# Self-attention on one core: key blocks met in a ring instead of a triangle, accumulation rounds dealt out beforehand, context products two steps late

## The chip, the cores and the metric

The kernel runs on one core of one Trainium2 chip. The metric is the device time of one execution in microseconds. The engines are PE (TensorE, matrix products; PEld is its weight load), DVE (VectorE), ACT (ScalarE), POOL (GpSimd) and SP (SyncE, which here issues every transfer between DRAM and SBUF). Each engine works through its own instructions in order and waits on semaphores of the others.

## The reference

The model takes four images of 128 channels and 64 x 64 positions through a mixer with convolutions and a state space scan, a convolution, then (on 4096 tokens of 128 channels per image) an attention with a small feed-forward part, an expert layer, a linear attention and a second expert layer. The change touches the first attention alone. Cut to what matters, it is, for x of shape (4, 4096, 128) with H = 16 heads of D = 8:

```python
qkv = _qz_ring(heads + rx_theta)            # running products of cosines, 8 numbers per token and head
q = jnp.transpose(qkv, (0, 2, 1, 3))        # (B, H, S, D)
scores = jnp.einsum('bhsd,bhtd->bhst', q, q) / np.sqrt(D)
attn = jax.nn.softmax(scores, axis=-1)
ctx = jnp.einsum('bhst,bhtd->bhsd', attn, q)
attn_out = ctx @ w_comb.T + b_comb
x1 = _ln(x + attn_out, g1, beta1)
zf = jnp.cos(x1[..., :NQ_FFN]) * jnp.cos(ry_theta)
h = jax.nn.relu(zf @ w1.T + b1)
ffn_out = h @ w2.T + b2
return _ln(x1 + ffn_out, g2, beta2)
```

Queries, keys and values are the same numbers, so the matrix of scores is symmetric: exp(score) of a block of queries against a block of keys, transposed, is that of the second block's queries against the first block's keys.

## The kernel before, in words

`layer2_attention` runs over the four images. For each one `prepare` computes q for all heads and stores it to DRAM (`head_d` for queries and keys, `value_d` for the values of the transposed half), while `feed_forward` finishes the image before. Then `attention` works alone. After the last image `feed_forward` runs by itself. What follows is `attention`.

The 4096 tokens make NJ = 4 blocks of 1024. In block j of head h, the queries of block j meet keys in steps: a step (h, j, m) takes the m-th pair of 128-key tiles, so m runs from 0 to 15 and m // 4 is the block of the keys. A step is *own* if m // 4 = j. If it lies in another block, it is called *met* here (`behind` in the code), and its exponentials are used twice. Block j meets all later blocks: block 0 has 12 met steps and 4 own ones, block 1 has 8 and 4, block 2 has 4 and 4, block 3 has only 4 own ones. `pairs` mixes them: in block 0 three met steps and an own one in turn, in block 1 two and one, in block 2 one and one. `blocks` puts block 3 of the head before between blocks 0 and 1. A head has 40 steps, 24 of them met.

One step does this, in the program's order:

- PE: four `score` products into two PSUM half-tiles (`sps`, L90 through the helper `mm`; the pool `pssc` has three half-tiles).
- PE: `turns(...)`, some *rounds* of products for the transposed half (`acc_ps`). A *group* is the four met steps of one (h, j, i), i being the block of the keys; its transposed exponentials fill a tile `turned` (two buffers), and eight rounds of four products each weigh them with the values of block j. `turns` computes at every step how many rounds are due (at least 1, at most 3) and stops if the group's last step is not two steps old. In the trace one product of these is two instructions, so a round is 8 instructions of `acc_ps`, and a step's context product 8 of `ctx_ps`.
- DVE: the second transpose of the met step before (L1197).
- PE: `weigh`, the context product of the step before: exp (`ex`) against the values `qt` into `ctx_ps`. At a block's end, for j > 0, it adds the transposed sums of earlier blocks by eight products with `place`; DVE copies ctx_ps (L1140), and SP stores it in eight transfers to `num_d` and `den_d`.
- DVE: sums of folded exponentials that are ready (L1204).
- ACT: two exps (L1211), each 128 x 1024. In a met step the row sums are needed too: either ACT writes them (`accum_out`, an extra read of its accumulator), or the step is put *aside*: POOL folds the exps twice (L1158, L1159) and DVE sums the rest. `folded` puts 11 of the 24 met steps aside.
- DVE: the first transpose of a met step (L1217).

The exps of a step lie in one of four buffers `ex`. A finished group's PSUM half is copied or added by DVE into `accs[h]` (L1089, L1091). When the last group of a block is done, the values of the block after next are loaded (`load_values`, four loads of L1022, tile `v`); three steps later POOL spreads them (`spread_values`, L1030, `turned_v`). The keys and queries of the next head come by 32 loads (L903) from block 1's first step on, and POOL rounds them (L912) 11 and 15 steps later.

PE, DVE and POOL keep the program's order in `attention`. The order of SP and ACT, and which of the four `ex` buffers a step gets, is decided by the framework's scheduler.

Of the kernel before, what the change touches and what calls it, by code (L numbers as in the profile page):

```python
# [17 lines left out]
P = 128  # L18
# [806 lines left out]
def layer2_attention(K, xd, dpool, w):  # L825
# [6 lines left out]
    with ExitStack() as ctx:  # L832
# [47 lines left out]
        head_d = dpool.tile([2, P, L], F32, name="head_d")  # L880
        value_d = dpool.tile([NH, 32, NJ - 1, 4, BT, HD], F32, name="value_d")
        num_d = dpool.tile([2, P, L], F32, name="num_d")
        den_d = dpool.tile([2, NH, L], F32, name="den_d")
        nrm_d = [dpool.tile([P, L], F32, name=f"nrm_d{i}") for i in range(2)]

# [28 lines left out]
        def prepare(b, big, two, work, psum):  # L914
# [50 lines left out]
            def store(c):  # L965
# [3 lines left out]
                j = c // 2  # L969
                if c % 2 == 0 and j < NJ - 1:  # L970
                    laters[j] = work.tile([P, NH, BT, HD], F32, name="later", bufs=1)
                if j < NJ - 1:
                    at = laters[j][:, :, 4 * (c % 2) : 4 * (c % 2) + 4]
                    nc.gpsimd.tensor_copy(at.rearrange("p h t d -> p t h d"), cs)
                if c % 2 and j < NJ - 1:
# [30 lines left out]
        def attention(qt, first, dsum, big, two, work, pssc, psctx, psacc):  # L1006
# [6 lines left out]

            dacc = big.tile([P, NJ - 1, NH, NTT], F32, name="dacc")
            nc.gpsimd.memset(dacc, 0.0)
# [33 lines left out]
            begins, last = {}, {}  # L1049
            for n, (h, j, _) in enumerate(steps):  # L1050
                begins.setdefault((h, j), n)
                last[h, j] = n
            heads = {0: first}
            values = {(0, 0): spread_values(load_values(0, 0))}
            waiting = []
            order = [(h, j) for h in range(NH) for j in range(NJ - 1)]
# [4 lines left out]
            halves = [0]  # L1061

            def turn():

                r, h, j, i, td, _, sums = groups[0]
                if r == 0:
# [15 lines left out]
                if r < BT - 1:  # L1082
                    return False
                groups.pop(0)
                if i == 1:
                    accs[h] = work.tile([P, NJ - 1, BT, 32], F32, name="acc")
                at = accs[h][:, i - 1]
                if j == 0:
# [3 lines left out]
                if i == NJ - 1:  # L1092
                    after = order.index((h, j)) + 2
                    if after < len(order):
                        waiting.append((now[0] + 3, order[after], load_values(*order[after])))
                return True

            def turns(n, ready):


                due = left = 0
                for g in groups:
                    left += BT - g[0]
                    due = max(due, -(-left // max(1, g[5] - n + 1)))
                for _ in range(min(max(due, 1), 3)):
                    if not groups or not ready(groups[0]) or turn():
                        return

            def weigh(h, j, m, exs):

                last = m == 4 * j + 3
                first = m == (4 * j + 4 if j < NJ - 1 else 4 * j)
                for p in range(2):
                    at = (h * NTT + 2 * m + p) * (HD + 1)
                    for c in range(2):
                        mm(
                            cps[unit(p, c), :],
                            qt[:, at : at + 32],
                            exs[:, p, c, :],
                            start=first,  # L1120
                            stop=last and j == 0,
                        )
                if not last:
                    return
                if j > 0:
                    while any(g[1] == h and g[3] == j for g in groups):
                        turn()
                    for k in range(2):
                        for p in range(2):
                            for c in range(2):  # L1130
                                a = 2 * p + k
                                mm(
                                    cps[unit(p, c), :].rearrange("r (t a s) -> r t a s", a=4, s=32)[:, :, a],
                                    place[:, a, :],
                                    accs[h][:, j - 1, 4 * c : 4 * c + 4],
                                    start=False,
                                    stop=k == 1,
                                )
# [8 lines left out]

            values[order[1]] = spread_values(load_values(*order[1]))
            folds = []

            def folded(j, m):

                return ((m - 4) % 3 == 0, m % 2 == 0, m % 4 < 3)[j]

# [8 lines left out]

            starts = [n for n, (h, j, m) in enumerate(steps) if m // 4 > j and m % 4 == 0]
            ends = dict(zip(starts, [n - 1 for n in starts[2:]] + [len(steps) - 1] * 2))
            begun = {}
            turned = None
            past = None
            now = [0]
            upright = None  # L1170
            for n, (h, j, m) in enumerate(steps):
                now[0] = n
                keys, queries = heads[h]
                if j in (1, 2) and h + 1 < NH:
                    at = n - begins[h, 1]
                    if at == 0:
                        heads[h + 1] = load(h + 1, two)
                    if at in (11, 15):
                        rounded(heads[h + 1][at == 15])
                while waiting and n >= waiting[0][0]:  # L1180
                    _, at, v = waiting.pop(0)
                    values[at] = spread_values(v)
                behind = m // 4 > j
                if n in ends:
                    turned = work.tile([P, BT, 2 * CH], F32, name="turned")
                    end = min(ends[n], last[h, m // 4])
                sps = [pssc.tile([P, 2, CH], F32, name="score") for p in range(2)]
                for p in range(2):
                    for c in range(2):
# [4 lines left out]
                        )  # L1194
                turns(n, lambda g: begun[id(g[4])] < n - 1)
                if upright is not None:
                    nc.vector.transpose(*upright)  # L1197
                    upright = None
                if past is not None:
                    weigh(*past)  # L1200

# [3 lines left out]
                exs = work.tile([P, 2, 2, CH], F32, name="ex", bufs=4)  # L1205
                aside = behind and folded(j, m)
                for p in range(2):
# [3 lines left out]
                    nc.scalar.activation(  # L1211
                        ex, sps[p], AF.Exp, scale=scale, accum_out=dacc[:, j, h, t : t + 1] if summed else None
                    )
# [4 lines left out]
                if aside:  # L1218
                    fold(n, exs, dacc[:, j, h, 2 * m : 2 * m + 2])
                past = (h, j, m, exs)  # L1220
                if behind and m % 4 == 3:
                    begun[id(turned)] = n
                    groups.append([0, h, j, m // 4, turned, end, None])
            assert upright is None and not groups
            weigh(*past)
            for _, qs, at in folds:
# [3 lines left out]
        def feed_forward(b, dsum, work, psum):  # L1230

            loads, x1s, hids, sums, halves, lasts, rcs = {}, {}, {}, {}, {}, {}, {}

            def fetch(c):
# [544 lines left out]
```

## Time and profile before

| | |
|---|---|
| time, three runs | 10711.77, 10717.14, 10717.62 us; median 10717.14 |
| profiled execution, span from first to last instruction | 10707.7 us (its own time is not listed apart; the median is 9.4 above the span) |
| busy in the span | PE 8939.2, DVE 7658.7, ACT 7518.8, POOL 5247.7 us |
| mean granted TensorE clock | 0.914; 1.00 in the attention stretches |
| attention stretches, from the first score that flows on | 3328.3 to 4689.2, 4904.6 to 6264.9, 6481.5 to 7839.8, 8055.4 to 9413.6 us |
| between them (`feed_forward` and the next `prepare`) | 215.2, 216.5 and 215.5 us |

In the lines of the profile, L12 is line 12 of the kernel, and L90 is the helper through which nearly all matrix products go, so that products are told apart by the tile they write (score, acc_ps, ctx_ps). A group's line gives out<-in, shapes, how many, then busy us, mean ns of one, and the idle time of its engine just before, with what ended it. A timeline's line gives start, length, engine, line, operation, how many, and in brackets the idle time before and what released it. Work of PE, PEld and ACT overlaps at its ends, so lengths add up to more than the time that passes: distances between starts are the surer measure.

### The profile page before, as it was taken

Reading aid. Unit: us, or ns where it says so; the run is one execution under the profiler, and the core shown is the slowest. Engines: PE = TensorE matmul, PEld = TensorE weight load, DVE = VectorE, ACT = ScalarE, POOL = GpSimd, SP = SyncE. Lnnn points to the kernel's source line nnn. Section 1 sums busy time; section 2 is a strip of 40 time slices with the busy share of each in tenths; the row PEclk is TensorE's granted clock in tenths of the full one; section 3 lists DMA queues with packets and bytes.
Section 4 is the critical chain, followed back from the end, with each engine's and each line's share of the span. In section 5 each row is a group of like instructions: output and inputs, shape, how many; then the busy total and the mean of one; then the engine's idle time right before and its main releaser. Section 6 shows DMA issues by size and latency. Waiting matters only on the chain. (4 is left out here: it accounts for less than half of the span.)

```text
span 10707.7 us, 184050 instructions
## 1 busy us (share of the span) xinstructions
PE 8939.2 (83%) x71952; PEld 3434.1 (32%) x71952; DVE 7658.7 (72%) x8462; ACT 7518.8 (70%) x10323; POOL 5247.7 (49%) x3143
## 2 busy tenths in 40 slices
PE   6777777777876999988999978999978999976767
PEld 2123323322342333333333333333333333323433
DVE  2788677668856777777777777777777777754563
ACT  3565575565536999977999968999968999941431
POOL 0565555456634666545556645666646665520000
PEclk8788888878888999999999989999989999987987
DMA  3322331322212122122122222222232222123004
GB/s 82 88 72 57 86 78 48 92 70 59 62 55 57 34 34 33 33 71 50 33 34 37 36 73 43 36 36 33 34 84 37 34 34 33 33 90 111 2 17 142
DMA packets 524325, 581.58 MB, mean 54 GB/s; under 512 B 106232, under 2 KB 329536, under 8 KB 520896
## 3 DMA queue, kind: packets, MB, share of 16 engines
q1 hardware_dynamic: 523456, 569.81, 23.3%
q8 instruction: 568, 9.31, 0.4%
q14 instruction: 301, 2.47, 0.1%
HBM read 373.96 MB, written 76.55 MB: 42 GB/s over the span
## 5 line engine op out<-in xcount | busy, mean ns | idle before, releaser
L1211 ACT ACTIVATE ex<-score 128x1024 f32<-128x1024 f32 x5120 | 4934.3, 1033 | 468.7 <-PE score L90 179.1
L90 PE MATMUL ctx_ps<-ex,qt 128*32 128x512 f32 x20480 | 2719.3, 595 | 0.0
L1158 POOL TENSOR_TENSOR folded<-ex 128x1024 f32<-128x1024 f32 x704 | 1680.1, 2387 | 2072.2 <-ACT ex L1211 2060.6
L1217 DVE STREAM_TRANSPOSE turned<-ex 128x1024 f32<-128x1024 f32 x1536 | 1880.1, 1224 | 499.2 <-ACT ex L1211 449.0
L90 PE MATMUL acc_ps<-turned,turned_v 128*32 128x256 f32 x24576 | 1826.2, 388 | 181.2 <-DVE turned L1197 179.7
L1197 DVE STREAM_TRANSPOSE turned<-ex 128x1024 f32<-128x1024 f32 x1536 | 1854.8, 1208 | 0.0
L90 PE MATMUL score<-queries,keys 32*128 32x512 f32 x10240 | 1357.8, 496 | 149.3 <-ACT ex L1211 83.6
L687 DVE TENSOR_TENSOR_SCAN hs<-decay,carry,hs 128x512 f32<-128x512 f32 x1024 | 1253.4, 1267 | 201.0 <-ACT decay L686 186.6
L686 ACT ACTIVATE decay<-dt,a_neg 128x512 f32<-128x512 f32 x1024 | 701.2, 690 | 793.2 <-DVE hs L687 769.9
L90 PEld LDWEIGHTS score<-queries,keys 32*128 32x128 f32 x10240 | 524.1, 182 | 2204.7 <-issue 1652.3
L693 POOL TENSOR_TENSOR hs<-hs,c_sb 128x1024 f32<-128x1024 f32 x512 | 1205.6, 2376 | 44.8 <-DMA c_sb<-c_d 25.3
L1159 POOL TENSOR_TENSOR quarters<-folded 128x512 f32<-128x512 f32 x704 | 906.0, 1287 | 55.2
L90 PEld LDWEIGHTS acc_ps<-turned,turned_v 128*32 128x32 f32 x24576 | 561.6, 108 | 897.7 <-issue 557.3
L90 PEld LDWEIGHTS ctx_ps<-ex,qt 128*32 128x32 f32 x20480 | 683.8, 109 | 461.6 <-DVE ctx L1140 53.3
L90 PE MATMUL y_ps<-hs,pair 128*64 128x512 f32 x2048 | 648.0, 756 | 135.5 <-POOL hs L693 135.2
L683 DVE TENSOR_TENSOR hs<-dtx,b_ps 128x2048 f32<-128x2048 f32 x256 | 582.6, 2276 | 248.5 <-PE b_ps L90 167.1
L1140 DVE COPY ctx<-ctx_ps 128x512 f32<-128x512 f32 x256 | 177.2, 692 | 669.7 <-PE ctx_ps L90 669.7
L690 POOL COPY carry<-hs 128x4 f32<-128x4 f32 x256 | 59.6, 233 | 1022.2 <-DVE hs L687 988.0
L1030 POOL TENSOR_TENSOR turned_v<-v,quarter 128x1024 f32<-128x1024 f32 x192 | 459.6, 2394 | 17.7 <-ACT ex L1211 11.2
L1204 DVE TENSOR_REDUCE dacc<-quarters 128x2 f32<-128x512 f32 x704 | 453.7, 644 | 7.3 <-POOL quarters L1159 7.3
L90 PE MATMUL b_ps<-dbc,spread 32*128 32x512 f32 x512 | 319.8, 707 | 69.0 <-DVE hs L683 69.0
L1211 ACT ACTIVATION_READ_ACCUMULATOR ex<-score 128x1 f32 x1664 | 348.5, 209 | 0.0
(353 smaller groups left out, 9505.2 us busy)
## 6 DMA issues: line engine op xcount, KB each, us to landing
c_sb<-c_d SPq DMA_DIRECT2D x512, 128.0 KB
queries<-head_d SPq DMA_DIRECT2D x1024, 64.0 KB
keys<-head_d SPq DMA_DIRECT2D x1024, 64.0 KB
dt<-dt SPq DMA_DIRECT2D x128, 256.0 KB
dtx<-dtx SPq DMA_DIRECT2D x128, 256.0 KB
w<-in_L_ffn_weight SPq DMA_DIRECT2D x32, 1024.0 KB
w<-in_L_ffn_weight SPq DMA_DIRECT2D x128, 256.0 KB
under<-xp SPq DMA_DIRECT2D x384, 66.0 KB
```

What stands on the lines that cost most here:

```text
L90: self.nc.tensor.matmul(out, lhsT, rhs, start=start, stop=stop)
L683: nc.vector.tensor_tensor(hs, dtx2, bb.unsqueeze(1).to_broadcast([P, NQ, CH]), ALU.mult)
L686: nc.scalar.activation(ex, dt2[:, q, :], AF.Exp, scale=a_neg[:, q, g : g + 1])
L687: nc.vector.tensor_tensor_scan(hs[:, q, :], ex, hs[:, q, :], carry[:, g, q : q + 1], ALU.mult, ALU.add)
L693: nc.gpsimd.tensor_tensor(at, at, cs.unsqueeze(1).to_broadcast([P, 2, CH]), ALU.mult)
L1030: nc.gpsimd.tensor_tensor(t, v.unsqueeze(2).to_broadcast([P, 4 * BT, 4, HD]), quarter.unsqueeze(1).to_broadcast([P, 4 * BT, 4, HD]), ALU.mult,
L1158: nc.gpsimd.tensor_tensor(hs, exs[:, :, 0], exs[:, :, 1], ALU.add)
L1159: nc.gpsimd.tensor_tensor(qs, hs[:, :, 0 : CH // 2], hs[:, :, CH // 2 :], ALU.add)
L1197: nc.vector.transpose(*upright)
L1204: nc.vector.tensor_reduce(at, qs, AX.X, ALU.add)
L1211: nc.scalar.activation(ex, sps[p], AF.Exp, scale=scale, accum_out=dacc[:, j, h, t : t + 1] if summed else None)
L1217: nc.vector.transpose(*upright)
```

## The change

The blocks meet in a ring: block 0 meets 1 and 2, block 1 meets 2 and 3, block 2 meets 3, block 3 meets 0. Every pair of blocks is still met once, and blocks 0 to 3 now have 8, 8, 4 and 4 met steps beside 4 own ones. The blocks of a head run in order, without the block of another head between them; each own step is followed by its share of met steps.

`rounds` is a table made beforehand: a group's eight rounds are spread evenly from three steps after its last score to the step in which the group after next begins to fill `turned`. `weigh` runs two steps late instead of one, and ahead of the rounds. Folding is done at m % 4 = 2, in blocks 2 and 3 at m % 4 = 0 too, 8 of 24 met steps.

The block pair (3, 0) gives its transposed sums to block 0, whose context has long been stored. These sums go to DRAM as a part of their own (`around_d`, 16 stores of 64 rows of 128 bytes per head), and `feed_forward` loads and adds them in its first two chunks of 512 tokens. `value_d` holds the values of block 3 too, and each head now loads and spreads values four times instead of three.

```diff
-        value_d = dpool.tile([NH, 32, NJ - 1, 4, BT, HD], F32, name="value_d")
+        value_d = dpool.tile([NH, 32, NJ, 4, BT, HD], F32, name="value_d")
...
+        around_d = dpool.tile([4, P, L // NJ], F32, name="around_d")
...
-            dacc = big.tile([P, NJ - 1, NH, NTT], F32, name="dacc")
+            meets = ((1, 2), (2, 3), (3,), (0,))
+            from_ = [[j for j in range(NJ) if i in meets[j]] for i in range(NJ)]
+            dacc = big.tile([P, 2, NH, NTT], F32, name="dacc")
...
-                later = list(range(4 * j + 4, NTT // 2))
-                n = len(later) // 4
+                own = list(range(4 * j, 4 * j + 4))
+                met = [m for i in meets[j] for m in range(4 * i, 4 * i + 4)]
+                n = len(met) // 4
                 for k in range(4):
-                    yield from later[n * k : n * k + n]
-                    yield 4 * j + k
-            blocks = [(h - (j == NJ - 1), j) for h in range(NH + 1) for j in (0, NJ - 1, *range(1, NJ - 1))]
-            steps = [(h, j, m) for h, j in blocks if 0 <= h < NH for m in pairs(j)]
+                    yield own[k]
+                    yield from met[n * k : n * k + n]
+            steps = [(h, j, m) for h in range(NH) for j in range(NJ) for m in pairs(j)]
...
+            rounds = [0] * (len(steps) + 16)
+            order = list(fills)
+            for k, (h, j, i) in enumerate(order):
+                at = fills[h, j, i][-1] + 3
+                to = fills[order[k + 2]][0] if k + 2 < len(order) else at + 5
+                if i > 0:
+                    to = min(to, last[h, i])
+                for x in range(BT):
+                    rounds[at + ((to - at + 1) * (x + 1) - 1) // BT] += 1
...
+                if i == 0:
+                    for g in range(4):
+                        for a in range(4):
+                            rows_ = slice(32 * g + HD * a, 32 * g + HD * a + HD)
+                            nc.sync.dma_start(
+                                out=around_d[g, HD * h : HD * h + HD].rearrange("d (t a r) -> d t a r", a=4, r=32)[:, :, a],
+                                in_=accs[h][rows_, 0],
+                            )
...
-                if j in (1, 2) and h + 1 < NH:
-                    at = n - begins[h, 1]
-                    if at == 0:
+                if h + 1 < NH:
+                    if n == begins[h, 1]:
                         heads[h + 1] = load(h + 1, two)
-                    if at in (11, 15):
-                        rounded(heads[h + 1][at == 15])
+                    if j == 2 and n - begins[h, 2] in (3, 7):
+                        rounded(heads[h + 1][n - begins[h, 2] == 7])
...
-                turns(n, lambda g: begun[id(g[4])] < n - 1)
                 if upright is not None:
                     nc.vector.transpose(*upright)
                     upright = None
-                if past is not None:
-                    weigh(*past)
+                if len(past) > 1:
+                    weigh(*past.pop(0))
+                for _ in range(rounds[n]):
+                    turn()
...
-                aside = behind and folded(j, m)
+                aside = behind and (m % 4 == 2 or m % 4 == 0 and len(meets[j]) == 1)
...
+            for n in range(len(steps), len(rounds)):
+                now[0] = n
+                if past:
+                    weigh(*past.pop(0))
+                for _ in range(rounds[n]):
+                    turn()
...
+                if c < CHB:
+                    part = arounds[c] = work.tile([P, 4, CH], F32, name="around", tag="hid")
+                    nc.sync.dma_start(out=part, in_=around_d[:, :, cols].rearrange("g q f -> q g f"))
...
+                if c in arounds:
+                    part = arounds.pop(c)
+                    nc.gpsimd.tensor_tensor(part[:, 0:2], part[:, 0:2], part[:, 2:4], ALU.add)
+                    nc.gpsimd.tensor_tensor(num, num, part[:, 0:2], ALU.add)
```

More of the change, by code (lines that the diff above doesn't have):

```diff
@@ L969, in store @@
                 j = c // 2
-                if c % 2 == 0 and j < NJ - 1:
+                if c % 2 == 0:
                     laters[j] = work.tile([P, NH, BT, HD], F32, name="later", bufs=1)
[L972 to L975, printed above, removed]
+                at = laters[j][:, :, 4 * (c % 2) : 4 * (c % 2) + 4]
+                nc.gpsimd.tensor_copy(at.rearrange("p h t d -> p t h d"), cs)
+                if c % 2:
                     for q in range(4):
@@ L1038, in pairs @@
             def pairs(j):
-                later = list(range(4 * j + 4, NTT // 2))
-                n = len(later) // 4
+                own = list(range(4 * j, 4 * j + 4))
+                met = [m for i in meets[j] for m in range(4 * i, 4 * i + 4)]
+                n = len(met) // 4
                 for k in range(4):
-                    yield from later[n * k : n * k + n]
-                    yield 4 * j + k
-            blocks = [(h - (j == NJ - 1), j) for h in range(NH + 1) for j in (0, NJ - 1, *range(1, NJ - 1))]
-            steps = [(h, j, m) for h, j in blocks if 0 <= h < NH for m in pairs(j)]
-            begins, last = {}, {}
-            for n, (h, j, _) in enumerate(steps):
+                    yield own[k]
+                    yield from met[n * k : n * k + n]
+            steps = [(h, j, m) for h in range(NH) for j in range(NJ) for m in pairs(j)]
+            begins, last, fills = {}, {}, {}
+            for n, (h, j, m) in enumerate(steps):
                 begins.setdefault((h, j), n)
                 last[h, j] = n
+                if m // 4 != j:
+                    fills.setdefault((h, j, m // 4), []).append(n)
+            rounds = [0] * (len(steps) + 16)
[7 more added lines that the diff above has]
+                    rounds[at + ((to - at + 1) * (x + 1) - 1) // BT] += 1
             heads = {0: first}
@@ L1055, in attention @@
             waiting = []
-            order = [(h, j) for h in range(NH) for j in range(NJ - 1)]
+            after = [(h, j) for h in range(NH) for j in range(NJ)]
             cps = psctx.tile([P, CH], F32, name="ctx_ps")
@@ L1061, in attention @@
             halves = [0]
+            now = [0]
             def turn():
-                r, h, j, i, td, _, sums = groups[0]
+                r, h, j, i, td, sums = groups[0]
                 if r == 0:
@@ L1082, in turn @@
                 if r < BT - 1:
-                    return False
+                    return
                 groups.pop(0)
[L1085 to L1088, printed above, removed]
+                if h not in accs:
+                    accs[h] = work.tile([P, NJ, BT, 32], F32, name="acc")
+                at = accs[h][:, i]
+                if j == from_[i][0]:
                     nc.vector.tensor_copy(at, sums)
@@ L1091, in turn, with weigh @@
                     nc.vector.tensor_tensor(at, at, sums, ALU.add)
[L1092 to L1112, printed above, removed]
+                if i == 0:
[6 more added lines that the diff above has]
+                            )
+                if i == meets[j][-1]:
+                    to = after.index((h, j)) + 2
+                    if to < len(after):
+                        waiting.append((now[0] + 3, after[to], load_values(*after[to])))
+            def weigh(n, exs):
+                h, j, m = steps[n]
                 for p in range(2):
@@ L1119, in weigh @@
                             exs[:, p, c, :],
-                            start=first,
-                            stop=last and j == 0,
+                            start=n == begins[h, j],
+                            stop=n == last[h, j] and j == 0,
                         )
-                if not last:
+                if n < last[h, j]:
                     return
                 if j > 0:
-                    while any(g[1] == h and g[3] == j for g in groups):
-                        turn()
                     for k in range(2):
@@ L1134, in weigh @@
                                     place[:, a, :],
-                                    accs[h][:, j - 1, 4 * c : 4 * c + 4],
+                                    accs[h][:, j, 4 * c : 4 * c + 4],
                                     start=False,
@@ L1146, in weigh @@
                         nc.sync.dma_start(out=den_d[p, h : h + 1, cols], in_=u[r + HD : r + HD + 1])
-            values[order[1]] = spread_values(load_values(*order[1]))
+            values[after[1]] = spread_values(load_values(*after[1]))
             folds = []
-            def folded(j, m):
-                return ((m - 4) % 3 == 0, m % 2 == 0, m % 4 < 3)[j]
             def fold(n, exs, at):
@@ L1160, in fold @@
                 folds.append((n + 3, qs, at))
-            starts = [n for n, (h, j, m) in enumerate(steps) if m // 4 > j and m % 4 == 0]
-            ends = dict(zip(starts, [n - 1 for n in starts[2:]] + [len(steps) - 1] * 2))
-            begun = {}
             turned = None
-            past = None
-            now = [0]
+            past = []
             upright = None
@@ L1182, in attention @@
                     values[at] = spread_values(v)
-                behind = m // 4 > j
-                if n in ends:
+                i = m // 4
+                behind = i != j
+                if behind and m % 4 == 0:
                     turned = work.tile([P, BT, 2 * CH], F32, name="turned")
-                    end = min(ends[n], last[h, m // 4])
                 sps = [pssc.tile([P, 2, CH], F32, name="score") for p in range(2)]
@@ L1205, in attention @@
                 exs = work.tile([P, 2, 2, CH], F32, name="ex", bufs=4)
-                aside = behind and folded(j, m)
+                aside = behind and (m % 4 == 2 or m % 4 == 0 and len(meets[j]) == 1)
+                if behind:
+                    sums = dacc[:, from_[i].index(j), h]
                 for p in range(2):
@@ L1211, in attention @@
                     nc.scalar.activation(
-                        ex, sps[p], AF.Exp, scale=scale, accum_out=dacc[:, j, h, t : t + 1] if summed else None
+                        ex, sps[p], AF.Exp, scale=scale, accum_out=sums[:, t : t + 1] if summed else None
                     )
@@ L1218, in attention @@
                 if aside:
-                    fold(n, exs, dacc[:, j, h, 2 * m : 2 * m + 2])
-                past = (h, j, m, exs)
+                    fold(n, exs, sums[:, 2 * m : 2 * m + 2])
+                past.append((n, exs))
                 if behind and m % 4 == 3:
[L1222 to L1225, printed above, removed]
+                    groups.append([0, h, j, i, turned, None])
+            nc.vector.transpose(*upright)
+            for n in range(len(steps), len(rounds)):
[4 more added lines that the diff above has]
+                    turn()
+            assert not groups and not past
             for _, qs, at in folds:
@@ L1230, in feed_forward @@
         def feed_forward(b, dsum, work, psum):
-            loads, x1s, hids, sums, halves, lasts, rcs = {}, {}, {}, {}, {}, {}, {}
+            CHB = NCH // NJ
+            loads, x1s, hids, sums, halves, lasts, rcs, arounds = {}, {}, {}, {}, {}, {}, {}, {}
             def fetch(c):
```

## The prediction

> **What bounds the kernel now.** I read the page first. Four stretches of about 1,360 us, the attention of four images, hold half of the 10707.7 us span, and three engines are nearly full in each (one stretch; columns: start and end, then busy us and instructions of PE, PEld, DVE, ACT, POOL, the granted clock, DMA share, GB/s):
>
> ```profile
> 6481.50:7839.80 1358.30, 1300.02 (x14586) 464.33 (x14586) 1062.06 (x1103) 1239.74 (x1695) 813.95 (x430) 1.00 0.20 33
> L1211 ACT ACTIVATE ex<-score 128x1024 f32<-128x1024 f32 x5120 | 4934.3, 1033 | 468.7 <-PE score L90 179.1
> ```
>
> Busy shares do not say who sets the pace, so I read the timeline step by step (start, length, engine, group):
>
> ```profile
> 4006.36 0.51 PE L90 MATMUL score<-queries,keys 32*128 32x512 f32 x4
> 4006.79 1.07 PE L90 MATMUL acc_ps<-turned,turned_v 128*32 128x256 f32 x16
> 4007.68 1.04 PE L90 MATMUL ctx_ps<-ex,qt 128*32 128x512 f32 x8
> 4008.65 0.50 PE L90 MATMUL score<-queries,keys 32*128 32x512 f32 x4
> 4009.08 0.64 PE L90 MATMUL acc_ps<-turned,turned_v 128*32 128x256 f32 x8
> 4009.54 1.04 PE L90 MATMUL ctx_ps<-ex,qt 128*32 128x512 f32 x8
> 4010.51 0.51 PE L90 MATMUL score<-queries,keys 32*128 32x512 f32 x4
> ```
>
> From one score to the next, a step with two rounds (16 instructions of acc_ps) takes 2.29 us, one with one round 1.86, one without 1.43: a step costs PE 1.43 + 0.433 per round. These values repeat to 0.01 us through all four stretches. `place` adds 0.44 (three times a head). A head has 40 steps and 48 rounds: 40 x 1.432 + 48 x 0.4325 + 3 x 0.44 = 79.4 us. The starts of score give 84.74 us per head in the steady state (52 heads). So PE sets the pace and waits 5.4 us per head. ACT passes at 0.92 us a plain exp and 1.00 with a read of the accumulator (five in 4.71 us, the last one 1.03 long; with the read, 4004.60 and then 4005.61 in the timeline): a step of 1.84 or 2.01.
>
> The waits stand at fixed steps (h, j, m): 0.75 us at (h, 0, 8) and (h, 0, 9) and 1.29 at (h, 0, 2), all in block 0 with its runs of three met steps; 0.74 at (h, 1, 12); 0.62 at (h, 2, 12), after a `place`; 1.83 at (h, 2, 11) and the step behind it. They sum to 5.2 of the 5.4. Two of them:
>
> ```profile
> 6809.54 0.50 PE L90 MATMUL score<-queries,keys 32*128 32x512 f32 x2
> 6809.73 1.02 ACT L1211 ACTIVATE ex<-score 128x1024 f32<-128x1024 f32 x1 [1.38 <-PE ctx_ps L90]
> ...
> 6810.90 0.50 PE L90 MATMUL score<-queries,keys 32*128 32x512 f32 x2 [0.86 <-ACT ex L1211]
> ...
> 6838.81 0.64 PE L90 MATMUL acc_ps<-turned,turned_v 128*32 128x256 f32 x8 [0.95 <-DVE turned L1197]
> ```
>
> The first three lines: the exp of (h, 2, 15) waits until the context matmuls before it end, since its `ex` tile is the one that they read; PE then waits for that exp. This wait is named 60 times (83.1 us of ACT). Last line: a round waits for DVE, whose transposes come every 1.13 us, so that a met step costs DVE 2.25 us and three in a row exceed what PE spends on them.
>
> **The change, part by part.** One profiled execution is summed; its span is 10707.7 us, and the median 10717.14 lies 9.4 above it, which I keep.
>
> Positions in the changed head count from 0 at its first step, (h, 0, 0).
>
> *Same work on PE.* Steps, rounds and places per head stay 40, 48 and 3. In the built order a head has 2 steps without a round, 28 with one and 10 with two: 2 x 1.43 + 28 x 1.866 + 10 x 2.296 + 3 x 0.44 = 79.4 again. Nothing is won but waits.
>
> *Ring and mixed steps.* No block has more than two met steps in a row: DVE 4 x 1.13 = 4.5 us against at least 5.6 of PE for two met steps and an own one. A group's rounds begin three steps after its last score. In the worst place (the step that copies both ctx and acc, position 13), DVE finishes the last transpose of the group (5,0,2) at about 4.0 us after that step's score, PE asks for it at 7.4. The 1.29, the 0.74 and the 0.75 go; the 0.62 returns as (a) below, and the 1.83 as (b).
>
> *Contexts two steps behind.* A context no longer asks for an exp that has just run; what it asks for now is 1.8 us older. Cost: `ex` is held a step longer, still within 4 buffers.
>
> *What is late next.* (a) Two steps without rounds now stand together at a head's start, position 0 and 1. The first context of a head must wait for DVE's copy of ctx_ps: copy 0.69 + 0.1 after `place`, of which 0.44 is covered by one score: 0.45 us with the lag of the semaphore. (b) In the built order the second exp of position 28, (h, 2, 10), waits for nothing more of PE, the mark that (h, 2, 15) had before: its first exp takes the `ex` of position 26 and so waits for weigh(26), 1.43 us after its score, where it would start 0.60-0.75 after. PE's next-but-one score then comes 0.48 late. (c) 0.07 at position 32, where ACT is 0.5 us behind. Together 1.0.
>
> *ACT.* Folds fall from 11 to 8 a head, so 3 steps go from 1.84 to 2.01: +0.5 us, 76.3 per head against PE's 79.4. Where one round meets an accumulating step, ACT falls 0.15 behind; steps with two rounds give 0.29 to 0.45 back. Bounds: with no slack between PE and ACT every step takes the longer of both: 81.5 plus (a) and (b) = 82.4 per head. With the slack that three score half-tiles give (0.44 us, worked out from the 0.60 start and the 0.92 exp), 80.4. Steps (h, 0, 13) to (h, 0, 15) before (a fold, then two accumulating steps, one round each) run at 1.86, 1.87, 1.86 with no stretch, so I stay near the lower end and add 0.5 for couplings that I can't see: 80.9. Saved: 84.74 - 80.9 = 3.84 us x 64 heads = 246 us (bounds 150 and 312, the latter with stalls of 0.5).
>
> *POOL* loses 3 x 3.67 us of folds a head and gains one spread of 2.39; a stretch falls from 814 us busy to 814 - 16 x 8.6 = 676.
>
> *SP.* 16 stores `around_d` per head are new, each of 64 rows of 128 B. In the built order they stand between the fifth and the sixth load of the next head's keys, so 27 loads (0.65 to 0.78 us each; 16 keys 11.11), eight ctx stores (2.4) and the four v loads of block 2 queue behind them:
>
> ```profile
> 6600.17 11.11 SPq L903 DMA_DIRECT2D keys<-head_d  x16
> 6611.64 11.83 SPq L903 DMA_DIRECT2D queries<-head_d  x16
> ...
> 6522.10 2.16 SPq L1022 DMA_DIRECT2D v<-value_d  x4
> ```
>
> From the score of position 7, where block (h-1, 3) ends its rounds: acc copied 2.8, then 16a, 27 x 0.70 = 18.9, 2.4, 1.7, about 2 to land: v is there at 27.8 + 16a us. No row shows a 64-row store; a v load of 32 rows has 0.42, a keys load 0.65: v lands at 34.5 to 38.2. POOL spreads it (2.39), then folds position 22 (2.39 + 1.29). DVE wants that fold at position 26 (40.4), so it may wait up to 4 us, but ACT needs the `ex` tiles of these folds only at positions 29, 30 and 33, where 38 is just in time. I take 0 on the path. The Trainium skill (DMA: Bandwidth & Descriptors, Specifications) speaks against this edit: it calls 512 B the least size for line rate, and its measured table gives 0.68 us for 4 KB in 64 packets. By that figure, as an estimate, a would be 0.68 and v would land at 38.7, on the edge, and the sum would be the same or some 30 us worse.
>
> *Between the stretches.* After the last place, 8 rounds remain on PE (3.5 us, the ctx stores lie beside them), then the acc copy and 16 stores go before the first den load. Before, that load was issued 4.4 us after the last matmul; now 0.5 + 16 x 0.42 + 1.3 = 8.5: +4 (to +8). Chunks 0 and 1 each add a 1 MB load and two POOL adds of 2.39 ahead of the sum of num, which had 2.7 us to spare in chunk 0: +4 (0 to +10). `later` for j = 3: two POOL copies of 0.61 and four stores, +1. About +10 per image, +40 in all (15 to 80); these sections are chains of waits at their start, so a late start moves the end.
>
> Sum: 10717 - 246 + 40 = 10511.
>
> **Rivals.**
> 1. *SP's queue makes it slower.* If a 128 B store costs more than 0.65 us, v lands after 38.2, POOL stands before the fold, `ex` comes free late and ACT stops. Every further us of landing is paid by each head. The gain of 206 us is 3.2 per head, so it turns at a landing of about 41.4, a = 0.85. For: the longest v, keys and queries loads took 1.6 to 1.9 us. Against: SP rows follow neither bytes nor rows strongly (0.26 to 0.78). At a = 1.0, 43.8: 5.6 x 64 = 358 lost, 10870.
> 2. *No slack between ACT and PE:* 82.4 per head, 150 - 40 = 110 saved, 10607. For: 16 reads of the accumulator instead of 13. Against: (h, 0, 13) to (h, 0, 15).
> 3. *The waits only move* (the change does not do what it says): DVE's copies, which wait for PE, hold back its transposes as before. 84.7 per head and +40: 10757. Against: DVE needs 64 of 80 us a head and each group has 3 us in hand.
>
> **How the numbers follow.** Forecast 0.70, rival 2 0.15, rival 1 0.09, rival 3 0.06 (half of it within the bound, since the sections may cost 15). The forecast's own range is 10420 (312 saved, +15) to 10600. The range to 10670 takes in rival 2 with sections at +80 and leaves out the slower cases and a tail below: about 0.2. A difference of 0.2%, 21 us, is about what a measurement of this kernel tells from none. Faster 0.86, same 0.04, slower 0.10.
>
> **What would show it.** Right: 80 to 81.5 us per head; steps of 1.86 and 2.29 almost throughout; no PE wait for `turned`; the ACT wait for ctx_ps once a head, at 0.8 us. Wrong: POOL's turned_v waiting for v<-value_d, or ACT's exp waiting for POOL folded; steps of 2.01 (rival 2); sections between the stretches beyond 235 us (now 215 to 217). The prediction falls if a head takes over 83.

## The result, and the profile after

The changed kernel takes 10786.92 us (median of four runs, 10779.16 to 10795.92) against 10717.38 for the kernel before: a ratio of 1.0066 with a 95% interval of 1.0052 to 1.0081. It is slower, by 70 us, where 206 us less were forecast.

The stretch that answers to the one shown of before (same columns), and from the page the shares by engine in the chain of work that ended last, first of the changed kernel, then of the kernel before:

```profile
6527.30:7883.00 1355.70, 1313.32 (x14586) 462.30 (x14586) 1036.77 (x1054) 1243.15 (x1791) 674.22 (x350) 0.98 0.21 36
```

```profile
PE 25%; SPq 8%; DMA 7%; DVE 5%; POOL 4%; issue 3%; ACT 2%; POOLq 0%; DVEq 0%; ACTq 0%
```

```profile
PE 13%; DVE 6%; DMA 2%; ACT 1%; SPq 1%; issue 1%; POOL 0%; DVEq 0%; ACTq 0%; POOLq 0%
```

POOL's busy time fell to 674 us, as worked out (676), and the stretch got shorter by only 2.6 us. The chain could be followed back over 54% of the span after and over 24% before, so its shares do not compare one to one; within the chain, SP's queue (SPq) has 8 parts of 54 where it had 1 of 24, and DMA 7 of 54 where it had 2 of 24. The granted clock of the stretch is 0.98 where it was 1.00, but, as the next paragraph shows, the steps that do not wait are as short as before: the clock is not what costs.

The starts of score, set against PE's own 1.432 us a step, 0.4325 a round and 0.44 a place, say where the time stands. Of the heads 1 to 14 (counted from 0) of the four stretches, a head takes 85.25 us on average (before 84.74), but from 81.6 to 89.0: the waits are no longer the same in each head. Outside seven positions the steps run at 1.43, 1.86 or 2.29. On average, what is over is 0.27 at position 1, 0.45 at position 2, 4.7 at positions 29 to 32, and 0.4 at position 34.

```text
sums in us, from the traces      before     after     change
four attention stretches         5434.4    5439.2       +4.8
three sections between them       647.4     704.9      +57.5
after the fourth stretch         1294.2    1308.9      +14.7
ahead of the first stretch       3331.8    3329.3       -2.5
```

(A stretch is counted in all kernels from its seventh score product, the first that finds no free half-tile and waits for an exp, to its last matmul. For the stretches behind the first, that is the start in the table of before.) So two things went wrong: the 246 us of expected gain became a loss of 5, and the sections and the part behind the fourth stretch cost 72 us instead of 40. One late head of the third stretch shows the first. SP's queue, from the around stores on; the score of position 7 is at 6784.55:

```profile
6787.43 11.54 SPq L1117 DMA_DIRECT2D around_d<-acc  x16
6799.01 7.59 SPq L904 DMA_DIRECT2D keys<-head_d  x11
6806.64 14.22 SPq L904 DMA_DIRECT2D queries<-head_d  x16
...
6826.97 1.82 SPq L1024 DMA_DIRECT2D v<-value_d  x4
```

POOL in the same head, then ACT, then PE (start, length, engine; in brackets the wait and what ended it):

```profile
6830.35 2.37 POOL L1032 TENSOR_TENSOR turned_v<-v,quarter 128x1024 f32<-128x1024 f32 x1 [21.20 <-DMA v<-value_d]
6832.68 2.33 POOL L1168 TENSOR_TENSOR folded<-ex 128x1024 f32<-128x1024 f32 x1
```

```profile
6828.80 1.94 ACT L1219 ACTIVATE ex<-score 128x1024 f32<-128x1024 f32 x2 [0.77 <-PE ctx_ps L90]
6835.05 1.94 ACT L1219 ACTIVATE ex<-score 128x1024 f32<-128x1024 f32 x2 [4.31 <-POOL folded L1168]
```

```profile
6831.73 0.50 PE L90 MATMUL score<-queries,keys 32*128 32x512 f32 x2
6836.12 0.79 PE L90 MATMUL score<-queries,keys 32*128 32x512 f32 x2 [3.89 <-ACT ex L1219]
```

Read from above: v is asked for 42.4 us after the score of position 7 and spread 45.8 us after it. POOL has stood before that spread for 21.20 us, and the fold of position 22, whose score began at 6814.68, comes right behind it. That fold ends at 6835.01; at 6835.05 ACT starts the exp that takes the tile which the fold was reading. PE waits 3.89 us for that exp. The list of waits shows the same for the whole run. Its second row is DVE, which sums what POOL has folded; that wait lies beside the chain, since PE's rounds wait only 3 us for `turned` in the whole run. In the kernel before, the three come to 6.6, 7.3 and 0 us:

```profile
POOL turned_v L1032 <- DMA v<-value_d: 562.8, 32, 22.3
DVE dacc L1210 <- POOL quarters L1169: 469.6, 168, 11.2
ACT ex L1219 <- POOL folded L1168: 185.1, 87, 5.4
```

The Trainium skill (Perfetto Trace Analysis, Tensor Engine Instruction) calls the execution queues of ACT, DVE and GpSimd strictly first in, first out; the two POOL rows above agree: POOL was idle for 21.20 us and began the fold only behind the spread.

Over 56 heads the spread starts 39.4 to 46.9 us after the score of position 7 (mean 42.9), and the lateness of the steps 29 to 32 follows it on a line: 1.03 us for each us, correlation 0.96. Drawn on, the line is at nothing at 38.3 and at 0.84 us at 39.1. The second is the better bound, because 0.84 us is lost at position 29 even when v is early (e1_one_store below).

The sections lose at their start. SP and POOL behind the third stretch, whose last matmul ends at 7882.95:

```profile
7883.46 11.19 SPq L1117 DMA_DIRECT2D around_d<-acc  x16
7896.24 0.32 SPq L1251 DMA_DIRECT2D den<-den_d  x1
```

```profile
7904.68 2.34 POOL L1265 TENSOR_TENSOR around<-around 128x1024 f32<-128x1024 f32 x1 [16.73 <-DMA x_in<-xd]
7907.10 2.34 POOL L1266 TENSOR_TENSOR num<-num,around 128x1024 f32<-128x1024 f32 x1
7909.52 1.26 POOL L1284 TENSOR_TENSOR num<-num 128x512 f32<-128x512 f32 x1
```

The first den load is issued 13.3 us after the last matmul (before 4.4), and the first sum of num ends 27.8 us after it (before 10.5, with 2.5 to spare for DVE). When the first store to nrm_d is issued, 36.7 us after the last matmul instead of 19.6, 17 of the 18 us by which this section is longer are there, and they stay.

### The profile page after: what moved, and what is told of

Read it like the earlier page. It is cut to its first block, busy times and chain, and to the rows that moved or that the text cites. A ratio compares the mean times of both kernels' runs of the same rounds, so it can differ in the third digit from the quotient of the medians.

```text
span 10782.3 us, 185075 instructions
## 1 busy us (share of the span) xinstructions
PE 9006.9 (84%) x71952; PEld 3429.7 (32%) x71952; DVE 7557.3 (70%) x8270; ACT 7532.1 (70%) x10707; POOL 4725.8 (44%) x2847
## 2 busy tenths in 40 slices
DMA packets 623021, 608.96 MB, mean 56 GB/s; under 512 B 192632, under 2 KB 424128, under 8 KB 619584
## 4 chain that ended last, share of the span: by engine, by line
PE 25%; SPq 8%; DMA 7%; DVE 5%; POOL 4%; issue 3%; ACT 2%; POOLq 0%; DVEq 0%; ACTq 0%
PE ctx_ps L90 9%; PE acc_ps L90 5%; SPq L1117 4%; PE score L90 4%; SPq L904 4%; DMA queries<-head_d 3%; POOL folded L1168 2%; DMA keys<-head_d 1%; PE ln_var L90 1%; DMA w<-in_L_ffn_weight 1%; POOL quarters L1169 1%; PE ln_xc L90 1%; PE kv L90 1%; PE hid_ps L90 1%; DMA v<-value_d 1%
## 5 line engine op out<-in xcount | busy, mean ns | idle before, releaser
L90 PE MATMUL ctx_ps<-ex,qt 128*32 128x512 f32 x20480 | 2763.4, 612 | 40.5 <-DVE ctx L1154 40.5
L1168 POOL TENSOR_TENSOR folded<-ex 128x1024 f32<-128x1024 f32 x512 | 1220.7, 2384 | 1517.6 <-ACT ex L1219 1484.4
L90 PE MATMUL score<-queries,keys 32*128 32x512 f32 x10240 | 1421.0, 501 | 237.4 <-ACT ex L1219 186.0
L90 PEld LDWEIGHTS acc_ps<-turned,turned_v 128*32 128x32 f32 x24576 | 805.5, 111 | 1498.9 <-issue 1338.1
L1032 POOL TENSOR_TENSOR turned_v<-v,quarter 128x1024 f32<-128x1024 f32 x256 | 611.3, 2389 | 1177.4 <-DMA v<-value_d 562.8
L1169 POOL TENSOR_TENSOR quarters<-folded 128x512 f32<-128x512 f32 x512 | 656.2, 1282 | 40.1
L1210 DVE TENSOR_REDUCE dacc<-quarters 128x2 f32<-128x512 f32 x508 | 334.2, 658 | 469.6 <-POOL quarters L1169 469.6
L90 PEld LDWEIGHTS ctx_ps<-ex,qt 128*32 128x32 f32 x20480 | 408.6, 109 | 683.0 <-issue 604.0
L1219 ACT ACTIVATION_READ_ACCUMULATOR ex<-score 128x1 f32 x2048 | 434.0, 212 | 0.0
L90 PEld LDWEIGHTS y_ps<-hs,pair 128*64 128x64 f32 x2048 | 142.1, 162 | 575.9 <-issue 290.9
```

The costliest lines, as they stand in the source:

```text
L90: self.nc.tensor.matmul(out, lhsT, rhs, start=start, stop=stop)
L1032: nc.gpsimd.tensor_tensor(t, v.unsqueeze(2).to_broadcast([P, 4 * BT, 4, HD]), quarter.unsqueeze(1).to_broadcast([P, 4 * BT, 4, HD]), ALU.mult,
L1168: nc.gpsimd.tensor_tensor(hs, exs[:, :, 0], exs[:, :, 1], ALU.add)
L1169: nc.gpsimd.tensor_tensor(qs, hs[:, :, 0 : CH // 2], hs[:, :, CH // 2 :], ALU.add)
L1219: nc.scalar.activation(ex, sps[p], AF.Exp, scale=scale, accum_out=sums[:, t : t + 1] if summed else None)
```

## The experiments

Theory: SP's queue makes v late, POOL stands before v in order, the folds behind it keep `ex` tiles, ACT and PE stop. First rival: the ring itself is bound by ACT, DVE or PE, and the late v hides it. Second rival: the 1024 short rows per head load the DMA engines, wherever the stores stand.

**e1_one_store.** `around_d` is laid out so that one store does what 16 did; the load follows the layout.

```diff
-around_d = dpool.tile([4, P, L // NJ], F32, name="around_d")
+around_d = dpool.tile([16, P, BT, 32], F32, name="around_d")
-for g in range(4):
-    for a in range(4):
...
+nc.sync.dma_start(
+    out=around_d[:, HD * h : HD * h + HD].rearrange("b d t r -> b d (t r)"),
+    in_=accs[h][:, 0].rearrange("p t r -> p (t r)"),
+)
...
+                        in_=around_d[:, :, 4 * c : 4 * c + 4].rearrange("b q t r -> q b (t r)"),
```

> The changed kernel with one around_d store of 128 rows of 1 KB per head in place of 16 stores of 64 rows of 128 B; the load in feed_forward becomes rows of 512 B; nothing is left out. Queue theory: in the changed kernel's trace v lands 39.4 to 46.9 us (mean 42.9) after the score of position 7, and the four steps 29 to 32 run 0.9 to 8.9 us late (mean 4.7), one us for each us of landing beyond 38.3. Fifteen stores of 0.71 us fewer bring the landing to 29 to 36, always below 38.3; what then stays is (a), 0.72, and about 1 at 29 to 34: 81 to 81.5 us per head, some 220 us saved against the kernel before. Sections between stretches lose about 10.5 of the 20 us that they gained: about +35 in all. Total 10530 (10490 to 10570). Rival 'the ring is bound by something else' (ACT, DVE or PE itself; the late v only hides it): heads stay above 84, total about 10740.

Measured: 10524.64 us, ratio to before 0.9818 (0.9803 to 0.9832). The spread starts at 28.5 to 35.2 us, heads take 80.97 (80.93 to 81.24), the stretches sum to 5198.6: 236 us less than before, where 246 was forecast. Sections take 227 (before 215 to 217, changed kernel 234 to 236). SP behind the third stretch:

```profile
7688.85 0.55 SPq L1114 DMA_DIRECT2D around_d<-acc  x1
7691.48 0.31 SPq L1248 DMA_DIRECT2D den<-den_d  x1
```

0.55 us stand where 11.19 stood. The first rival falls: with v in time, the ring runs as costed. POOL still stands before spreads for v (303.6 us in the list of waits of this kernel); begun by 35.2, they cost PE nothing, so that wait alone is no sign of a loss. What is left over PE's 79.4 is 0.27 and 0.45 at positions 1 and 2, and 0.84 at position 29.

**e2_stores_late.** The 16 stores as they are (put into `store_around`), issued later, for the head before.

```diff
+if kept and n - begins[h, 0] == 34:
+    store_around()
```

> The changed kernel with its 16 stores per head as they are, but issued at position 34 of the next head, behind the v loads of block 2, not ahead of the key and query loads; nothing is left out. Queue theory: what counts is the place in SP's queue; v lands as in the one-store kernel, heads 81 to 81.5 us; the sections keep their +20, since the last head's stores still stand ahead of the den load: 10717 - 220 + 77 = 10575 (10530 to 10620). Rival 'traffic': the 1024 rows of 128 B load the DMA engines wherever the stores stand, and other loads land as late as now: 10740 to 10800.

Measured: 10555.1 us, 0.9848 (0.9833 to 0.9863). Heads take 80.97, and the sections 235, as in the changed kernel. So the late v alone is worth 232 us (10786.92 - 10555.1). The packets are those of the changed kernel (192,633 under 512 B; 192,632 there), so the second rival falls: the place in SP's queue counts, not the traffic.

**e12_spread_late.** The changed kernel with its stores untouched; POOL's instruction is moved, not the load.

```diff
-waiting.append((now[0] + 3, after[to], load_values(*after[to])))
+waiting.append((now[0] + (12 if after[to][1] == 2 else 3), after[to], load_values(*after[to])))
```

> The changed kernel with all its 16 stores where they are, and one thing moved: POOL's spread of v for block 2 stands 12 steps behind the end of its group, not 3, so the folds of positions 22, 25 and 29 stand ahead of it in POOL's queue. v still lands at about 43 us after the score of position 7. If the late v costs time because POOL stands before it with the folds (and so ex tiles) behind: PE first needs this v at position 34 (some 52 us), the waits of 29 to 32 go, heads 80 to 81; sections stay +20: 10500 to 10560. If the late v itself, or the DMA traffic of the stores, is what stops the head: 10740 to 10790.

Measured: 10501.12 us, 0.9796 (0.978 to 0.9813): below even the one-store kernel. Heads take 80.09, sections 232 to 238. SP and POOL in a head whose position 7 is at 6466.10:

```profile
6508.60 1.69 SPq L1024 DMA_DIRECT2D v<-value_d  x4
```

```profile
6505.00 2.38 POOL L1168 TENSOR_TENSOR folded<-ex 128x1024 f32<-128x1024 f32 x1 [1.93 <-DVE ctx L1154]
...
6513.34 2.38 POOL L1168 TENSOR_TENSOR folded<-ex 128x1024 f32<-128x1024 f32 x1 [2.76 <-ACT ex L1219]
...
6518.88 2.38 POOL L1032 TENSOR_TENSOR turned_v<-v,quarter 128x1024 f32<-128x1024 f32 x1
```

v is issued 42.5 us after position 7, as late as in the head shown above, and PE does not wait: the folds are done, and the spread, 52.8 us after position 7, waits for nothing. So here the late landing cost only through what was queued behind the instruction that waits for it. SP's load and POOL's order are both needed for the loss; taking away either is enough.

Of the 5.2 us per head that this edit saves, 0.84 are the wait at position 29, which is gone too and has another cause (e13_best below). So the edit also changed which `ex` tile an exp takes. That the rest is POOL's order, and not the tiles, rests on the rows of the late head, in which the exp begins when the fold ends (6835.01, then 6835.05).

**e3_before_two_behind.** The kernel before, with contexts two steps late and nothing else.

```diff
-if past is not None:
-    weigh(*past)
+if len(past) > 1:
+    weigh(*past.pop(0))
```

> The kernel before with one part of the change alone: contexts two steps behind, order and rounds as before. If the 1.83 us per head at (h, 2, 11) and the step behind it is the context asking for an exp that has just run, it goes: 64 x 1.8 = 117 saved, 10600 (10580 to 10640). If the waits only move (to DVE's transposes, which come late in block 0): 10700 to 10717.

Measured: 10715.06 us, 0.9994 (0.9985 to 1.0004): no difference. PE's wait at (h, 2, 11) goes from 1.49 to 0.06, and 1.26 appears one step earlier, at (h, 2, 15). ACT's wait for contexts is as it was (83.0 us, 60 times; before 83.1, 60 times); in one head of the third stretch it reads

```profile
6816.50 2.86 ACT L1211 ACTIVATE ex<-score 128x1024 f32<-128x1024 f32 x3 [1.39 <-PE ctx_ps L90]
```

In both kernels the exp that waits takes an `ex` tile whose context has just run. So the distance of the context does not make this wait. The choice of the tile, which the scheduler makes, is what is left; no run changes it alone.

**e4_one_behind.** The one-store kernel with contexts one step late.

```diff
-if len(past) > 1:
+if past:
     weigh(*past.pop(0))
```

> The one-store kernel with contexts one step behind, as in the kernel before: this part of the change undone. If contexts two behind are needed, the own step's exp waits for the context matmuls again, as in (h, 2, 15) before, at least once and up to four times a head: 60 to 250 us above the one-store kernel. If the mixed order alone removes the waits: within 20 us of it.

Measured: 10911.11 us, 1.018 (1.0165 to 1.0195): 386 above the one-store kernel, dearer than expected. Heads take 87.26; 0.4 us or so is lost at nearly every own step. From its list of waits (PE's weight load for a context waits for the exp):

```profile
PEld ctx_ps L90 <- ACT ex L1216: 212.4, 728, 0.4
```

**e9_one_behind_rounds_first.** The same, with the step's rounds ahead of its context.

```diff
+for _ in range(rounds[n]):
+    turn()
 if past:
     weigh(*past.pop(0))
-for _ in range(rounds[n]):
-    turn()
```

> The kernel with contexts one step behind (10911), with the rounds of a step ahead of its contexts, as they stood in the kernel before. In its trace PE's contexts wait for an exp that has just run, about 0.4 us at each own step; a round of 0.43 ahead of them lets that exp end. If the place within the step is what makes one step behind so dear: 10540 to 10640. If the distance itself does: 10850 to 10911.

Measured: 10542.41 us, 0.9843 (0.9828 to 0.9857), heads 81.45. With the rounds first, two steps late is worth only some 18 us by the medians and 27 by the stretches; it was needed because the change put the context ahead of the rounds, where it reaches PE before its exp is done.

**e5_chunk_order.** The one-store kernel, in which `feed_forward` takes its chunks in another order.

```diff
+order = (*range(CHB, NCH - CHB), *range(CHB), *range(NCH - CHB, NCH))
+return in_turn(NCH, *(lambda k, f=f: f(order[k]) for f in stages))
```

> The one-store kernel with the feed-forward's chunks taken in the order 2, 3, 4, 5, 0, 1, 6, 7, so that the two chunks with an around load and two POOL adds do not come first; nothing is left out. In the one-store trace the sections between stretches take 231 us (218 to 219 before): the first num waits for the around load (8.4 us to land) and two adds (4.8). If that chain at the section's start is the cost: sections 219 to 224, the attention unchanged at 1295 a stretch, some 30 to 45 us saved: 10485 (10475 to 10500). If the section is bound by work that the two chunks add wherever they stand (POOL, DMA): 10515 to 10530.

Measured: 10492.21 us, 0.9792 (0.9778 to 0.9807); sections 218 to 221, attention 5197.8. (The expectation counts sections from later scores, and not from the same one in both kernels: its 231 is 227 here, its 218 to 219 are 215 to 217.) The chain at the section's start was most of the cost; some 4 us a section over before's 215 to 217 remain, which were not traced further.

**e7_early_round.** The one-store kernel with a round at position 1.

```diff
-at = fills[h, j, i][-1] + 3
+at = fills[h, j, i][-1] + (2 if i == 0 else 3)
```

> The one-store kernel with the rounds of each group (h, 3, 0) dealt out from two steps after its last score, not three, so that position 1 of the next head gets a round. Theory (a): at position 2 PE waits 0.45 us for DVE's copy of ctx_ps, since only one score stands between; a round of 0.43 behind the place covers it: 64 x 0.43 = 27 us less, head 80.5, 10497. Rival: the round at position 1 waits for DVE's last transposes, and the wait only moves: 10520 to 10530.

Measured: 10494.15 us, 0.9796 (0.9781 to 0.981). The 0.45 at position 2 is gone, heads take 80.55: (a) was what it was said to be.

**e8_all.** Both of these, and a fifth `ex` tile. Three `quarters` tiles in place of six make the room, so DVE sums as soon as more than two folds wait, not five.

```diff
-qs = work.tile([P, 2, CH // 2], F32, name="quarters", bufs=6)
+qs = work.tile([P, 2, CH // 2], F32, name="quarters", bufs=3)
...
-exs = work.tile([P, 2, 2, CH], F32, name="ex", bufs=4)
+exs = work.tile([P, 2, 2, CH], F32, name="ex", bufs=5)
```

> The one-store kernel with the chunk order and the early round of the two other kernels, and with five ex tiles in place of four (three quarters tiles in place of six make the room). Theory (b): the second wait of a head, 0.84 us at position 29, is the exp of position 28 that must wait for the contexts of position 26 to free its ex tile; a fifth tile takes it away: 64 x 0.84 = 54 us. Sum: 10525 - 40 - 27 - 54 = 10404 (10390 to 10440). If the wait of (b) has another cause, it stays: 10458.

Measured: 10471.52 us, 0.9772 (0.9756 to 0.9788), 67 above the sum. The 0.84 at position 29 is gone and stands at 31. ACT at that place in the one-store kernel, and in this one:

```profile
6850.13 6.52 ACT L1216 ACTIVATE ex<-score 128x1024 f32<-128x1024 f32 x7 [0.77 <-PE ctx_ps L90]
```

```profile
6839.37 2.86 ACT L1216 ACTIVATE ex<-score 128x1024 f32<-128x1024 f32 x3 [0.89 <-PE ctx_ps L90]
```

In the built program the exp of position 30 takes the tile of position 28 although there are five: the scheduler chooses the tile, not the order of the steps. (The tile's number is not in the traces; they show that the exp waits for a context.) That the scheduler counts the tile of position 22 as held, by a fold behind a spread that it expects late, is a guess; the next kernel fits it.

**e13_best.** One store, chunk order, early round and late spread, with four `ex` tiles.

> The one-store kernel with the chunk order, the early round and the late spread (four ex tiles, as in the changed kernel). In the kernel with five tiles the wait of 0.84 us moved from position 29 to 31, since the exp there took the tile of two steps before, freed just then; in this build no exp from 22 to 33 takes a tile younger than four steps. If that is (b): head 79.7, 10492 - 27 - 54 = 10411 (10395 to 10440). If (b) has another cause: 10455 to 10475.

Measured: 10406.78 us, 0.9703 (0.9689 to 0.9718), the fastest version: 380 us less than the changed kernel and 315 less than the kernel before in the same comparison, by the medians. Its third stretch, with sections of 218 to 221 beside it:

```profile
6325.03:7605.30 1280.27, 1279.17 (x14586) 449.96 (x14586) 1035.79 (x1054) 1235.08 (x1791) 676.22 (x350) 1.00 0.22 38
```

Heads take 79.65 (79.62 to 79.79); the 0.84 is gone and 0.27 at position 1 is all that is left over PE's 79.4. So (b) is a wait for the tile, as named, and moving the spread ends it; by which rule the scheduler then chooses stays open.

## Why the prediction was wrong

**The step that failed** is the SP term, "I take 0 on the path". It cost 232 us (the changed kernel against e2_stores_late). Its deadline and its price were near: 38.2 was the highest landing taken to be without loss (measured 39.1), and "Every further us of landing is paid by each head" (measured 1.03). The landing was mis-sized. It was put at 34.5 to 38.2 and is 42.9 on average, counted to the start of the spread, by these terms:

```text
                                  forecast        measured, mean of 56 heads
acc copied, first store           2.8             2.9
16 around stores                  6.7 to 10.4     11.4 (0.71 each)
27 key and query loads            18.9            20.4 (7.8 and 12.6)
ctx stores ahead of v             2.4             4.6 (2.8 to 7.0)
v issued and landed               3.7             3.6
```

With 42.9, 3.8 us beyond 39.1, the price gives 3.9 us per head, and with the 0.84 of position 29 the steps 29 to 32 lose the 4.7 that were measured. Two habits lie under the wrong size. The store's price was bounded from above by the length of a keys load, 0.65, while the same sum counts that load at 0.70, from start to start; the store is 0.656 long (median) and takes 0.71 from start to start. The Trainium skill's 0.68 (DMA: Bandwidth & Descriptors, Bandwidth), which was weighed there, came nearer than the 0.65, but by luck: it is the busy time of the DMA engines for a load that GpSimd issues, not the time that a store holds SP's queue. And 27 x 0.70 came from one head. The trace of before had dearer ones, and they were there to be read; the query loads of two other heads of that kernel:

```profile
6781.42 15.25 SPq L903 DMA_DIRECT2D queries<-head_d  x16
7374.22 14.53 SPq L903 DMA_DIRECT2D queries<-head_d  x16
```

The whole batches of 16 query loads in that stretch run from 11.4 to 15.3 us: 11.83 was near the low end, and 16 x 0.70 = 11.2 lies below them all. Where a deadline is missed or met by one us, the mean and the tail of a term count, not a typical head.

**Rival 1** is what came, by its own mechanism, though not at its own point: it asked for a store above 0.65, and for 0.85 to end slower. At 0.71 it ended slower, since the loads and ctx stores behind the stores were dearer too. It had a chance of 0.09. Its turning point of 41.4 us of landing was close: 236 us saved with v in time, less 72 for the sections, is 2.6 us a head, which beyond 39.1 gives 41.7. The measured 42.9 lies beyond both.

**Right.** The attention itself: 80.9 us per head forecast, 80.97 with v in time. (a) was 0.45 and measured 0.45; (b) was 0.48 and measured 0.84; (c) was 0.07 and is not there; the 0.5 for couplings that could not be seen became 0.27 at position 1. That these misses cancel to 0.07 is in part luck. No group waits for DVE's transposes, and ACT had the slack that rival 2 denied it: the steps that read the accumulator run at 1.86. Rival 3 falls with the one-store kernel.

**Right in kind, too small:** the sections, 72 us instead of 40 (the upper end was 80). The stores cost 11.2 us ahead of the den load instead of 6.7, and the around load landed late and had two adds behind it.

**Half right:** contexts two steps late were taken to end the wait of 1.83. Alone they end nothing (e3); in the ring they were needed for another reason, the new order within a step (e4, e9).

## What to carry to other kernels

When a change adds transfers to a queue, sum the whole queue up to the load that matters from the mean and the longest of each term over all heads, and take a deadline that is met by one or two us as missed. Then look at who waits for that load: put the waiting instruction behind the work that doesn't need it, as late as its first reader allows, before making the load faster; here one number in one line was worth 286 us, some 54 of them by way of (b) (0.84 x 64). And look at the DRAM layout, which the kernel is free to choose: here it alone made the difference between 16 short stores and one.

## What the hardware showed that was not expected

- A store of 64 rows of 128 B holds SP's queue 0.71 us; one store with the same data, 128 rows of 1 KB, is 0.56 us long (median), less than a single one of the 16 (0.656).
- In the one-store kernel the six loads of x_in that stand right behind an around load (2048 rows of 512 B) held SP's queue for 3.99 to 4.66 us, where 0.43 is the median of all; in the changed kernel, whose around load has 512 rows of 2 KB, it was 0.50 to 1.15. The batches of query loads and the ctx stores behind them vary too. That an issue waits for transfers ahead of it fits this, but was not tested alone.
- The part ahead of the first attention stretch, which the experiments left alone, took 3325.1 to 3348.3 us in the profiled executions. So the sums above compare stretches and sections, not spans.
